# Aggregating the edges of 32 targets in half of the PE's columns, two batches side by side

## The chip, the cores and the metric

The kernel runs on one core of one Trainium2 chip. The metric is the device time of one launch in microseconds (us), the median of several runs. A profile of one execution of the kernel before is at hand. Its engines are called PE (matmul), PEld (PE's weight loads), DVE, ACT, POOL and SP.

## The reference

A gated graph layer over 16 batches (b), 1024 nodes and 256 channels. `adj` is a sparse 1024 x 1024 matrix, used as both A_a and A_m, with some 9 sources u per target v:

```python
pre_u = einsum('bud,dk->buk', h, W1[:d]);  pre_v = einsum('bvd,dk->bvk', h, W1[d:])
S   = sigmoid(relu(pre_u[:, :, None] + pre_v[:, None] + b1) @ W2 + b2)     # per edge (u, v)
a_t = einsum('buv,bud->bvd', S * A_a, h)
m_t = einsum('uv,bud->bvd', A_m, h) * h
z   = beta1 * h + beta2 * (a_t @ Wa + ba) + beta3 * (m_t @ Wm + bm)
```

Only the pairs (u, v) where `adj` is not zero matter, so the kernel works on a list of edges.

## The kernel before

The work is cut into 4 groups of 4 batches (`GB = 4`) and 8 blocks of 128 targets: 32 blocks `k`. A block has two windows of 64 targets (`W`), and the edges of a window lie packed in 5 tiles (`TW`) of 128 slots, one edge per slot and partition. So there are 320 tiles, 10 steps `s` per block.

**Lists.** For each of the 8 target blocks `lists(vt)` loads a 128 x 1024 piece of the transposed matrix (`key`), finds each target's sources, and gives each edge a slot. `ahead` is a matrix of ones and zeros whose product with the counts gives each target its first slot. `LO = [0, 6, 20, 32, 32]` says which 32 targets (`V`) tile j may serve; `since` and `until` bound the slots of each target accordingly. The results are `uidx` (the row to gather), `val` (the edge's weight), `onehot` (which of the tile's 32 targets the slot belongs to) and `whose` (target by slot, written by four DMAs per list from the SP queue). Lists 0 to 2 are made before the first tile, lists 3 to 7 are drawn out over blocks 0 to 4, one piece per step.

**Per tile n.** `fetch` gathers 128 rows of a table in DRAM into one of five buffers: 4 batches of pre_u, then 4 batches of h (8 KB a row). `expand` puts pre_v of each edge's target into PSUM (`pc`). `gate` adds the two on DVE, does relu, the product with W2 and the sum over channels; ACT makes the sigmoid and four weighted copies `left[:, 1 + b]`, beside `left[:, 0]`, the ungated weight (`left_adj`). `aggregate` multiplies: the stationary operand is 128 channels of h of the fetched rows, the moving one the 2 x 32 columns of `left` (ungated and gated). There are 8 such products per tile, 4 batches by 2 halves of the channels, and the sums stand in PSUM as `acc`, channels on partitions.

**Per window and block.** `window_end` copies `acc` to `LT` with two ACT copies, and `times_h` multiplies the ungated half by h on DVE. In the next block's steps 2 to 5 `block_end` multiplies `LT` by Wm and Wa, adds the row of biases and h, and writes the result out.

**Beside that**, PE makes, for later blocks, pre_u rows (`rows`, L319 with w_u) and pre_v with its halves swapped (`halves`, L319 with w_v and L360).

**Order.** The order on each engine is the order in which the code is written: the loop over n at the end issues `aggregate(n - 1)`, then the fetches, then `gate(n)`, `left_adj(n + 1)`, then what is due, a piece of a list, and pieces of `block_end`, `halves` and `rows` at fixed steps s, and last `expand(n + 2)`. Small PSUM results share two buffers "misc"; `pc` has two buffers, `acc` one.

Of the kernel before, what the change touches and what calls it, by code (L numbers as in the profile page):

```python
# [13 lines left out]
P = 128  # L14
# [3 lines left out]
def kernel(  # L18
# [37 lines left out]


    nc = tc.nc
    B, N, D = x.shape
# [10 lines left out]
    V = 32  # L70
    LO = [0, 6, 20, 32, 32]
    RC = 5 + S
# [53 lines left out]
    until = fixed([P, 1], "until")  # L126
    hit = fixed([P, 1], "hit")
    nc.vector.memset(since, 0.0)
    nc.vector.memset(until, float(P))
    for lo in LO[1:]:  # L130
        nc.vector.tensor_scalar(hit, inw, float(lo), float(P), ALU.is_ge, ALU.mult)
        nc.vector.tensor_tensor(until, until, hit, ALU.add)
    for lo in LO[:-1]:
        nc.vector.tensor_scalar(hit, inw, float(lo + V), float(P), ALU.is_ge, ALU.mult)
        nc.vector.tensor_tensor(since, since, hit, ALU.add)

    ahead = fixed([P, P], "ahead")
    nc.vector.tensor_scalar(ahead[:, :W], upto[:, :W], row, None, ALU.is_gt)
    nc.vector.tensor_scalar(ahead[:, W:], upto[:, W:P], row, late, ALU.is_gt, ALU.mult)
    slot_of = fixed([P, NW, TW], "slot_of")  # L140
# [6 lines left out]
    nc.vector.tensor_scalar(ident, upto[:, :P], row, None, ALU.is_equal)  # L147
    place = fixed([P, NW, TW, V], "place")
    for w in range(NW):
        for j in range(TW):  # L150
            nc.vector.tensor_scalar(place[:, w, j, :], upto[:, :V], float(LO[j]), None, ALU.add)
    slot, nth = upto, upto[:, :S]
# [18 lines left out]
    val = const.tile([P, NT * NW, TW], FP, name="val")  # L171
    onehot = const.tile([P, NT * NW, TW, V], mybir.dt.bfloat16, name="onehot")
    whose = const.tile([P, NT * NW, E], mybir.dt.uint8, name="whose")
# [24 lines left out]
    def lists(vt):  # L198
# [21 lines left out]
        pw = aside(vt)  # L220
        nc.tensor.matmul(pw[:, 0:1], ahead, R[:, 0:1], start=True, stop=True)
        yield
        first = R[:, 1:2]
        nc.vector.tensor_copy(first, pw[:, 0:1])
# [4 lines left out]
        nc.vector.scalar_tensor_tensor(held, first, since, held, ALU.is_ge, ALU.mult)  # L229
        nc.vector.tensor_tensor(R[:, 0:1], held, first, ALU.add)  # L230
# [14 lines left out]
        for w, mine in enumerate((soon, late)):  # L245
            nc.vector.tensor_scalar(RR[:, w, :], R, mine, None, ALU.mult)
            for h in range(2):
                nc.sync.dma_start(whose[h * W:(h + 1) * W, vt * NW + w, :], few[w * W:(w + 1) * W])
        pe = aside(vt)
        for j in range(TW):  # L250
# [20 lines left out]
        nc.vector.tensor_scalar(vidx[:, sl].rearrange("p w j -> p (w j)"), k_of, BIG + N, None, ALU.add)  # L271
        nc.vector.tensor_tensor(onehot[:, sl].rearrange("p w j v -> p (w j) v"),  # L272
                                place.rearrange("p w j v -> p (w j) v"),
                                L[:, :, 4:5].to_broadcast([P, M, V]), ALU.is_equal)
        wanted.extend((i, j) for i in range(vt * NW, (vt + 1) * NW) for j in range(TW))
# [186 lines left out]

    marks, pcs, accs, hbs, LTs, lefts = {}, {}, {}, {}, {}, {}

# [20 lines left out]
    def left_adj(n):  # L485
        k, g, vt, w, j = where(n)
        i = vt * NW + w
        lefts[n] = wk.tile([P, 1 + GB, V], FP, name="left")
        nc.scalar.activation(lefts[n][:, 0, :], onehot[:, i, j, :], AF.Copy, scale=val[:, i, j:j + 1])  # L489

    def gate(n):
# [10 lines left out]
        for b in range(GB):  # L502
            nc.scalar.activation(lefts[n][:, 1 + b, :], lefts[n][:, 0, :], AF.Copy, scale=gt[:, b:b + 1])  # L503

    def aggregate(n):
        k, g, vt, w, j = where(n)
        if j == 0:
            accs[n // TW] = psa.tile([P, GB, DC, 2, W], FP, name="acc")
        left, f, acc = lefts.pop(n), fetched[n % NF], accs[n // TW]
        for b in range(GB):  # L510
            for c in range(DC):
                d = GD + b * D + c * P
                nc.tensor.matmul(acc[:, b, c, :, LO[j]:LO[j] + V], f[:, d:d + P], left[:, 0:b + 2:b + 1, :],  # L513
                                 start=(j == 0 and b % 2 == 0 and c == 0), stop=(j == TW - 1),
                                 skip_group_check=True)

    def window_end(q, step):
        k, w = divmod(q, NW)
        acc = accs.pop(q)
        if w == 0:  # L520
            LTs[k] = big.tile([P, GB * DC, 2, P], FP, name="LT")
        LT = LTs[k]
        v = slice(w * W, (w + 1) * W)
        for h in range(2):
            i = slice(h * GB * DC // 2, (h + 1) * GB * DC // 2)
            nc.scalar.copy(LT[:, i, :, v], acc[:, h * GB // 2:(h + 1) * GB // 2].rearrange("p b c k v -> p (b c) k v"))  # L526

        def times_h():
            nc.vector.tensor_tensor(LT[:, :, 0, v], LT[:, :, 0, v],  # L529
                                    hTs[k].rearrange("p b c n -> p (b c) n")[:, :, v], ALU.mult)  # L530
            if w == NW - 1:
                del hTs[k]
        after(step + 1, times_h)

    def block_end(k):
# [3 lines left out]
        for h in range(2):  # L539
            for bb in range(2):  # L540
                step = yield
                if bb == 0:
                    pz = small("pz")
                    add_row(pz, bias_p)
                b = 2 * h + bb
                for i, wt in enumerate((w_m, w_a)):
                    for c in range(DC):
                        nc.tensor.matmul(pz[:, bb * D:(bb + 1) * D], LTs[k][:, b * DC + c, i, :], wt[:, c, :],  # L548
                                         start=False, stop=(i == 1 and c == DC - 1), skip_group_check=True)
# [21 lines left out]
    for n in range(total + T):  # L571
# [19 lines left out]
        if 0 < n < total:  # L591
            next(more, None)
        if s in (2, 3, 4, 5) and 0 < k <= BS:
            if s == 2:
# [134 lines left out]
```

## Time and profile before

| what | value |
|---|---|
| median of 3 runs | 1355.8 us (1355.45 to 1357.64) |
| the profiled execution | 1355.8 us, its span 1353.9 us |
| busy time in the span | PE 1277.7, PEld 1167.6, DVE 1096.4, ACT 753.4, POOL 435.1 us |
| mean granted PE clock | 0.953 |
| moved by DMA | 389.34 MB, 296.70 MB of it by the gathers |

The span runs from the first to the last instruction. Busy time is the time in which at least one instruction of the engine ran. A matmul's recorded duration reaches over the start of the next one, so the pace of PE is read from the chain of work (the work that ended last, followed back), whose pieces do not overlap. In a group of instructions the columns are: line, engine, operation, written and read tiles, shape, count; then busy time in us and the mean of one in ns; then the engine's idle time before them, and what ended most of it.

The slices of the span show three stages: set-up until the first gate at about 90 us; blocks 0 to 4 until about 340 us, with the remaining lists; and an even stretch after that.

```profile
PE   5658999888999999999999999999999999999997
...
DVE  9539789888778888888887888888887888888874
ACT  2325455454556656556655665655655666666652
```

### The profile page before, as it was taken

How to read it: one execution, taken by the hardware profiler on the slowest of the kernel's cores; microseconds unless marked ns; L12 is line 12 of the kernel's file. 1: busy time of each engine (PE TensorE's matmuls, PEld its weight loads, DVE VectorE, ACT ScalarE, POOL GpSimd, SP SyncE). 2: the span in 40 equal slices, each digit the busy share in tenths (PEclk: the TensorE clock that was granted, in tenths of full speed). 3: DMA queues.
4: the chain of work that ended last, by engine and by line, in shares of the span. 5: the costliest groups of instructions: out<-in, count | busy, mean ns of one | idle time of the engine just before them, and what ended most of it. 6: DMA issues, size and time to landing. Idle time of an engine off the chain costs nothing.

```text
span 1353.9 us, 24556 instructions
## 1 busy us (share of the span) xinstructions
PE 1277.7 (94%) x8096; PEld 1167.6 (86%) x8096; DVE 1096.4 (81%) x3413; ACT 753.4 (56%) x2434; POOL 435.1 (32%) x411
## 2 busy tenths in 40 slices
PE   5658999888999999999999999999999999999997
PEld 4548888777999999999999999999999999999986
DVE  9539789888778888888887888888887888888874
ACT  2325455454556656556655665655655666666652
POOL 2047534443432222222222222222222333333320
PEclk9776978898999999999999999999999999999988
DMA  7687867767899998888899998988998888888872
GB/s 225 204 266 248 277 213 231 268 243 262 279 328 323 329 320 306 315 310 303 311 327 329 329 318 307 318 314 298 314 319 291 313 300 298 298 303 309 305 279 73
DMA packets 143304, 389.34 MB, mean 288 GB/s; under 512 B 16336, under 2 KB 101840, under 8 KB 106960
## 3 DMA queue, kind: packets, MB, share of 16 engines
q0 software_dynamic: 48640, 296.70, 62.1%
q1 hardware_dynamic: 75392, 72.62, 16.3%
q10 hardware_dynamic: 19136, 18.35, 4.4%
q8 instruction: 66, 1.08, 0.3%
q14 instruction: 70, 0.57, 0.1%
HBM read 391.69 MB, written 50.33 MB: 326 GB/s over the span
## 4 chain that ended last, share of the span: by engine, by line
PE 66%; DVE 12%; issue 8%; DMA 7%; POOL 3%; ACT 2%; SPq 1%; ACTq 0%; POOLq 0%; DVEq 0%
PE acc L513 29%; PE misc L548 13%; PE misc L319 12%; PE pc L481 8%; DVE t L498 4%; DMA fetched<-table,uidx 4%; DVE t L494 3%; POOL fetched L467 2%; PE misc L323 2%; DMA key<-in_adjT_dram 2%; DVE R L210 1%; POOL val L282 1%; PE misc L360 1%; DMA table<-in_x_dram 1%; ACT LT L526 1%
## 5 line engine op out<-in xcount | busy, mean ns | idle before, releaser
L513 PEld LDWEIGHTS acc<-left,fetched 128*128 128x128 f32 x5120 | 637.0, 196 | 50.6 <-ACT left L503 23.8
L513 PE MATMUL acc<-left,fetched 128*128 128x64 f32 x5120 | 625.2, 277 | 15.4 <-ACT left L503 15.4
L467 POOL DMA_INDIRECT fetched<-table,uidx x320 | 339.8, 1062 | 827.2 <-PE acc L513 613.9
L494 DVE TENSOR_TENSOR t<-fetched,pc 128x1024 f32<-128x1024 f32 x320 | 389.0, 1216 | 130.2 <-PE pc L481 74.2
L498 DVE SCALAR_TENSOR_TENSOR t<-t,w_b 128x256 f32<-128x256 f32 x1280 | 470.3, 422 | 23.9 <-ACT LT L526 0.5
L503 ACT ACTIVATE left<-left,gt 128x32 f32<-128x32 f32 x1280 | 306.5, 310 | 10.4
L481 PE MATMUL pc<-X,mark 128*128 128x512 f32 x640 | 251.9, 475 | 19.6 <-DVE t L494 18.1
L501 ACT ACTIVATE gt<-sc,b_b 128x4 f32<-128x4 f32 x320 | 95.4, 298 | 187.0 <-DVE t L498 186.1
L526 ACT COPY LT<-acc 128x512 f32<-128x512 f32 x128 | 68.7, 589 | 216.5 <-PE acc L513 216.5
L481 PEld LDWEIGHTS pc<-X,mark 128*128 128x128 f32 x640 | 123.0, 196 | 37.5 <-DVE t L494 20.2
L319 PE MATMUL misc<-w_u,hT 128*128 128x256 f32 x512 | 136.5, 416 | 17.8 <-DMA hT<-in_xT_dram 9.5
L548 PE MATMUL misc<-w_m,LT 128*128 128x256 f32 x512 | 140.3, 398 | 1.6 <-DVE LT L529 1.6
L548 PE MATMUL misc<-w_a,LT 128*128 128x256 f32 x512 | 135.9, 389 | 0.0
L319 PEld LDWEIGHTS misc<-w_u,hT 128*128 128x128 f32 x512 | 100.9, 207 | 33.1 <-ACT tab L335 10.1
L319 PE MATMUL misc<-w_v,hT 128*128 128x256 f32 x512 | 122.7, 383 | 0.0
L548 PEld LDWEIGHTS misc<-w_a,LT 128*128 128x128 f32 x512 | 100.5, 196 | 14.5
L319 PEld LDWEIGHTS misc<-w_v,hT 128*128 128x128 f32 x512 | 99.0, 193 | 13.1
L548 PEld LDWEIGHTS misc<-w_m,LT 128*128 128x128 f32 x512 | 96.0, 198 | 12.2 <-DVE LT L529 1.9
L282 POOL DMA_INDIRECT val<-in_adjT_dram,vidx x80 | 85.3, 1066 | 59.6 <-DVE onehot L272 36.1
L498 DVE DVE_READ_ACCUMULATOR t<-t,w_b 128x1 f32 x1280 | 104.0, 81 | 0.0
L335 ACT COPY tab<-misc 128x512 f32<-128x512 f32 x64 | 37.4, 585 | 115.8 <-PE misc L319 101.0
L489 ACT ACTIVATE left<-onehot,val 128x32 f32<-128x32 bf16 x320 | 97.7, 305 | 0.0
(104 smaller groups left out, 662.2 us busy)
## 6 DMA issues: line engine op xcount, KB each, us to landing
hT<-in_xT_dram SPq DMA_DIRECT2D x32, 512.0 KB, 7.7
table<-in_x_dram ACTq DMA_DIRECT2D x32, 512.0 KB, 8.2
table<-tab SPq DMA_DIRECT2D x32, 512.0 KB, 7.9
h_blk<-in_x_dram SPq DMA_DIRECT2D x32, 512.0 KB, 12.7
out_dram<-h_blk SPq DMA_DIRECT2D x32, 512.0 KB, 4.8
fetched<-table,uidx POOLq DMA_INDIRECT x320, 7.5
key<-in_adjT_dram SPq DMA_DIRECT2D x8, 512.0 KB, 9.6
whose<-few SPq DMA_DIRECT2D x32, 40.0 KB, 3.5
```

Source lines behind the costliest of these rows:

```text
L282: nc.gpsimd.indirect_dma_start(out=val[:, i, j:j + 1], out_offset=None, in_=adj_flat, in_offset=bass.IndirectOffsetOnAxis(ap=vidx[:, i, j: ...
L319: nc.tensor.matmul(p[:, bb * D:(bb + 1) * D], hT[:, 2 * h + bb, i, :], wt[:, i, :], start=(i == 0 and not begun), stop=(i == DC - 1), skip ...
L467: nc.gpsimd.indirect_dma_start(out=fetched[n % NF], out_offset=None, in_=table[g], in_offset=bass.IndirectOffsetOnAxis(ap=uidx[:, vt * NW ...
L481: nc.tensor.matmul(pcs[n][:, c], marks[n // TW][:, j * P:(j + 1) * P], cuts[k][:, w, c], start=True, stop=True)
L489: nc.scalar.activation(lefts[n][:, 0, :], onehot[:, i, j, :], AF.Copy, scale=val[:, i, j:j + 1])
L494: nc.vector.tensor_tensor(t, fetched[n % NF][:, :GD].rearrange("p (b d) -> p b d", b=GB), pcs.pop(n).rearrange("p (b d) -> p b d", b=GB), ...
L498: nc.vector.scalar_tensor_tensor(t[:, b, :], t[:, b, :], 0.0, w2_b, ALU.max, ALU.mult, accum_out=sc[:, b:b + 1])
L501: nc.scalar.activation(gt, sc, AF.Sigmoid, bias=b2_b)
L503: nc.scalar.activation(lefts[n][:, 1 + b, :], lefts[n][:, 0, :], AF.Copy, scale=gt[:, b:b + 1])
L513: nc.tensor.matmul(acc[:, b, c, :, LO[j]:LO[j] + V], f[:, d:d + P], left[:, 0:b + 2:b + 1, :], start=(j == 0 and b % 2 == 0 and c == 0), s ...
L526: nc.scalar.copy(LT[:, i, :, v], acc[:, h * GB // 2:(h + 1) * GB // 2].rearrange("p b c k v -> p (b c) k v"))
L548: nc.tensor.matmul(pz[:, bb * D:(bb + 1) * D], LTs[k][:, b * DC + c, i, :], wt[:, c, :], start=False, stop=(i == 1 and c == DC - 1), skip_ ...
```

## The change

1. **Which tiles serve which targets.** The lower 32 targets of a window are packed from slot 0 up and may use tiles 0 to 2; the upper 32 from slot 640 down, tiles 4 to 2. `HALVES` names the halves a tile serves: one, except tile 2, which serves both. `onehot` so has 6 parts of 32 per window in place of 5.
2. **Aggregation.** The operands change places. The stationary one is now 64 columns (32 targets, ungated and gated) of `left`, the moving one 256 channels of a batch. Batches 0 and 1 write partitions 0 to 63 of PSUM (columns 0 to 63 of PE), batches 2 and 3 partitions 64 to 127; they are issued in the order 0, 2, 1, 3. A tile has 4 products, tile 2 has 8. Each half has a PSUM accumulator of its own (`acc0`, `acc1`).
3. **Sums transposed.** The sums now stand with targets on partitions. `half_end` copies an accumulator to SBUF on ACT (`ev`) when its last tile is done; `turn_over` transposes it on PE by four matmuls with the unit matrix into "misc", and ACT copies that to `LT`. This stands at steps 7 (both halves of the first window), 9, and 1 of the next block. `LT` has one buffer in place of two.
4. **Steps moved.** `block_end` runs at steps 3 to 6 in place of 2 to 5, `halves` at 0, 2, 3, 4, 7 in place of 0, 1, 3, 6, 7.
5. **`left`** holds the ungated weights once per batch, beside the gated ones, so that 64 columns lie together; `left_adj` writes 128 columns (256 for tile 2) in place of 32.
6. **The four `whose` DMAs** of a list are issued from ACT's queue in place of SP's.

```diff
-    LO = [0, 6, 20, 32, 32]
+    HALVES = [[0], [0], [0, 1], [1], [1]]
+    OFF = [0, V, 2 * V, 4 * V, 5 * V, 6 * V]
...
+    nc.vector.tensor_scalar(until, upper, float((TW - 1 - MID) * P), float((MID + 1) * P), ALU.mult, ALU.add)
+    nc.vector.tensor_scalar(since, upper, float(MID * P), None, ALU.mult)
+    nc.vector.tensor_scalar(base, upper, float(E), None, ALU.mult)
...
         nc.tensor.matmul(pw[:, 0:1], ahead, R[:, 0:1], start=True, stop=True)
+        nc.tensor.matmul(pw[:, 1:2], below, R[:, 0:1], start=True, stop=True)
...
-                nc.sync.dma_start(whose[h * W:(h + 1) * W, vt * NW + w, :], few[w * W:(w + 1) * W])
+                nc.scalar.dma_start(whose[h * W:(h + 1) * W, vt * NW + w, :], few[w * W:(w + 1) * W])
...
-        lefts[n] = wk.tile([P, 1 + GB, V], FP, name="left")
-        nc.scalar.activation(lefts[n][:, 0, :], onehot[:, i, j, :], AF.Copy, scale=val[:, i, j:j + 1])
+        m = len(HALVES[j])
+        lefts[n] = wk.tile([P, m, GB, 2, V], FP, name=f"left{m}", bufs=3 if m == 1 else 1)
+        nc.scalar.activation(lefts[n][:, :m, :, 0, :],
+                             onehot[:, i, OFF[j]:OFF[j + 1]].rearrange("p (q v) -> p q v", q=m).unsqueeze(2)
+                             .to_broadcast([P, m, GB, V]), AF.Copy, scale=val[:, i, j:j + 1])
...
-        for b in range(GB):
-            for c in range(DC):
-                d = GD + b * D + c * P
-                nc.tensor.matmul(acc[:, b, c, :, LO[j]:LO[j] + V], f[:, d:d + P], left[:, 0:b + 2:b + 1, :],
-                                 start=(j == 0 and b % 2 == 0 and c == 0), stop=(j == TW - 1),
+        for i, q in enumerate(HALVES[j]):
+            first = j == (MID if q else 0)
+            if first:
+                accs[q] = psa.tile([P, 2, D], FP, name=f"acc{q}")
+            for b in (0, 2, 1, 3):
+                half, pair = divmod(b, 2)
+                nc.tensor.matmul(accs[q][half * 2 * V:(half + 1) * 2 * V, pair, :],
+                                 left[:, i, b].rearrange("p k v -> p (k v)"), f[:, GD + b * D:GD + (b + 1) * D],
+                                 start=(first and pair == 0), stop=(j == (TW - 1 if q else MID)),
...
-    def window_end(q, step):
...
+    def half_end(n, q):
+        evs[q] = one.tile([P, 2, D], FP, name=f"ev{q}")
+        nc.scalar.copy(evs[q], accs.pop(q))
+
+    def turn_over(k, w, q, step):
...
+        pt = small("pt")
+        ev = evs.pop(q)
+        for i in range(4):
+            pair, c = divmod(i, DC)
+            nc.tensor.transpose(pt[:, i * P:(i + 1) * P], ev[:, pair, c * P:(c + 1) * P], ident)
+        v = slice(w * W + q * V, w * W + (q + 1) * V)
+        nc.scalar.copy(LT.rearrange("p a c b k v -> p (a c b k) v")[:, :, v], pt.rearrange("p (i v) -> p i v", v=V))
...
-            if n % TW == 0:
-                window_end(n // TW - 1, n)
+            if n % TW in (0, MID + 1):
+                half_end(n - 1, 0 if n % TW else 1)
...
+        if s == 1 and k > 0:
+            turn_over(k - 1, 1, 1, n)
-        if s in (2, 3, 4, 5) and 0 < k <= BS:
+        if s in (3, 4, 5, 6) and 0 < k <= BS:
...
+        if s == 7 and k < BS:
+            turn_over(k, 0, 0, n)
+            turn_over(k, 0, 1, n)
+        if s == 9 and k < BS:
+            turn_over(k, 1, 0, n)
-        if k + 1 < BS and s in (0, 1, 3, 6, 7):
+        if k + 1 < BS and s in (0, 2, 3, 4, 7):
```

**Where instructions stand on PE.** Each row is line, operation, written and read tiles, shape, count; one product is one matmul here. Before, around the middle of a block (fetched0 to fetched4 are the five gather buffers, mark and X the operands of `expand`, LT, w_m and w_a those of `block_end`):

```order
L548 MATMUL misc<-w_m,LT 128x256 x2
L548 MATMUL misc<-w_a,LT 128x256 x2
L481 MATMUL pc<-X,mark 128x512 x2
L513 MATMUL acc<-left,fetched_184 128x2x32 x8
L323 MATMUL misc<-bias_p,unit 128x512
L548 MATMUL misc<-w_m,LT 128x256 x2
L548 MATMUL misc<-w_a,LT 128x256 x2
L481 MATMUL pc<-X,mark 128x512 x2
L513 MATMUL acc<-left,fetched_186 128x2x32 x8
```

After, the last step of `block_end` and step 7 with its transposes (ev and ident), then the tile that serves both halves:

```order
L582 MATMUL misc<-w_m,LT 128x256 x2
L582 MATMUL misc<-w_a,LT 128x256 x2
L500 MATMUL pc<-X,mark 128x512 x2
L537 MATMUL acc_9515<-fetched_173,left_9503 64x256 x4
L556 MATMUL misc<-ident,ev_9420 128x128 x4
L556 MATMUL misc<-ident,ev_9488 128x128 x4
L379 MATMUL misc<-low,swap 128x512
L500 MATMUL pc<-X,mark 128x512 x2
L537 MATMUL acc_9515<-fetched_175,left_9536 64x256 x4
L537 MATMUL acc_9594<-fetched_175,left_9536 64x256 x4
```

Eight products of a tile have become four of another shape, or eight for tile 2, between the same neighbours, and transposes stand at four places of a block.

**On SP's queue**, in blocks 1 and 2 (key is the input of the next list, h_blk and out_0_dram a block's h and result, tab a piece of the gather table). Before:

```order
L555 DMA out_0_dram<-h_blk_623 128x4x256
L248 DMA whose_148<-few_1456 64x640 x4
L200 DMA key_1553<-in_adjT_dram 128x1024
L576 DMA h_blk_1564<-in_x_dram 128x4x256
L336 DMA table1_61<-tab_1505 128x1024
```

After:

```order
L589 DMA out_0_dram<-h_blk_628 128x4x256
L212 DMA key_1554<-in_adjT_dram 128x1024
L610 DMA h_blk_1571<-in_x_dram 128x4x256
L355 DMA table1_61<-tab_1509 128x1024
```

The four `whose` DMAs, which read ACT's `few`, no longer stand between a block's output and the next list's key.

More of the change, by code (lines that the diff above doesn't have):

```diff
@@ L124 @@
     nc.vector.scalar_tensor_tensor(inw, late, -float(W), row, ALU.mult, ALU.add)
[L125 to L139 removed]
+    upper = fixed([P, 1], "upper")
+    nc.vector.tensor_scalar(upper, inw, float(V), None, ALU.is_ge)
+    lower = fixed([P, 1], "lower")
+    nc.vector.tensor_scalar(lower, inw, float(V), None, ALU.is_lt)
+    MID = TW // 2
+    until = fixed([P, 1], "until")
+    nc.vector.tensor_scalar(until, upper, float((TW - 1 - MID) * P), float((MID + 1) * P), ALU.mult, ALU.add)
+    since = fixed([P, 1], "since")
+    nc.vector.tensor_scalar(since, upper, float(MID * P), None, ALU.mult)
+    base = fixed([P, 1], "base")
+    nc.vector.tensor_scalar(base, upper, float(E), None, ALU.mult)
+    ahead = fixed([P, P], "ahead")
+    below = fixed([P, P], "below")
+    hv = fixed([P, 2 * NW, 1], "hv")
+    for q in range(2 * NW):
+        nc.vector.tensor_tensor(hv[:, q, :], late if q // 2 else soon, upper if q % 2 else lower, ALU.mult)
+    nc.vector.memset(below, 0.0)
+    for q in range(2 * NW):
+        c = slice(q * V, (q + 1) * V)
+        nc.vector.tensor_scalar(ahead[:, c], upto[:, c], row, hv[:, q, :], ALU.is_le if q % 2 else ALU.is_gt, ALU.mult)
+        if q % 2:
+            nc.vector.tensor_scalar(ahead[:, c], ahead[:, c], -1.0, None, ALU.mult)
+            nc.vector.tensor_copy(below[:, c], hv[:, q - 1, :].to_broadcast([P, V]))
     slot_of = fixed([P, NW, TW], "slot_of")
@@ L147 @@
     nc.vector.tensor_scalar(ident, upto[:, :P], row, None, ALU.is_equal)
[L148 to L151, printed above, removed]
+    place = fixed([P, 2, V], "place")
+    nc.vector.tensor_copy(place.rearrange("p k v -> p (k v)"), upto[:, :W])
     slot, nth = upto, upto[:, :S]
@@ L221, in lists @@
         nc.tensor.matmul(pw[:, 0:1], ahead, R[:, 0:1], start=True, stop=True)
+        nc.tensor.matmul(pw[:, 1:2], below, R[:, 0:1], start=True, stop=True)
         yield
         first = R[:, 1:2]
-        nc.vector.tensor_copy(first, pw[:, 0:1])
+        nc.vector.tensor_tensor(first, pw[:, 0:1], base, ALU.add)
+        from_ = wk.tile([P, 1], FP, name="from", bufs=2)
+        nc.vector.tensor_tensor(from_, pw[:, 1:2], since, ALU.max)
         held = wk.tile([P, 1], FP, name="held", bufs=2)
@@ L510, in aggregate @@
[L510 to L522 removed]
+        left, f = lefts.pop(n), fetched[n % NF]
@@ new lines, in half_end @@
+    def half_end(n, q):
+        evs[q] = one.tile([P, 2, D], FP, name=f"ev{q}")
+        nc.scalar.copy(evs[q], accs.pop(q))
+    def turn_over(k, w, q, step):
+        if w == 0 and q == 0:
+            LTs[k] = one.tile([P, 2, DC, 2, 2, P], FP, name="LT")
+        LT = LTs[k]
+        pt = small("pt")
[5 more added lines that the diff above has]
+        nc.scalar.copy(LT.rearrange("p a c b k v -> p (a c b k) v")[:, :, v], pt.rearrange("p (i v) -> p i v", v=V))
+        if not q:
+            return
```

34 lines of the change are left out of this document (16 added, 18 removed).

## The prediction

> **What bounds the kernel now.** I read the page's busy times first, then the chain of work, first over blocks 8 to 20 and then piece by piece over one block, and last the groups by line. (Names: a block is 10 gather tiles; there are 32.)
>
> ```profile
> span 1353.9 us, 24556 instructions
> ...
> PE 1277.7 (94%) x8096; PEld 1167.6 (86%) x8096; DVE 1096.4 (81%) x3413; ACT 753.4 (56%) x2434; POOL 435.1 (32%) x411
> ```
>
> ```profile
> 90.00:340.00 250.00, 224.75 (x1246) 199.94 (x1247) 217.08 (x660) 123.86 (x389) 128.45 (x121) 0.84 0.75 250
> 378.00:867.00 489.00, 489.00 (x3244) 453.29 (x3244) 398.76 (x1251) 295.69 (x974) 138.11 (x131) 1.00 0.90 318
> 1056.00:1315.00 259.00, 257.62 (x1728) 238.75 (x1727) 226.01 (x718) 162.49 (x545) 80.69 (x75) 0.98 0.85 303
> ```
>
> The second fence has three windows (length, then busy time of PE, PEld, DVE, ACT, POOL, granted clock, DMA share, GB/s): blocks 0 to 4, blocks 8 to 20 (13 of them, 37.6 us each) and blocks 24 to 31. From 378 us on PE is never idle and DVE is busy 82%; in blocks 0 to 4 PE and DVE share the bound and the clock is 0.84. The chain says the same and prices each kind of PE work:
>
> ```profile
> by line: PE acc L513 45.9%; PE misc L548 18.7%; PE misc L319 18.7%; PE pc L481 12.3%; PE misc L323 3.0%; PE misc L360 1.5%
> ```
>
> ```profile
> 810.28 1.78 PE misc L548 x8
> 812.06 0.46 PE pc L481 x2
> 812.52 1.73 PE acc L513 x16
> 814.25 0.29 PE misc L323
> 814.54 1.73 PE misc L548 x8
> ```
>
> The first fence is the chain of blocks 8 to 20 by line: all of it is PE, and 45.9%, 17.3 us per block, the aggregation at L513. The rows of the second (start, us) are one tile's step. An aggregation costs 1.73 us in 16 records, 108 ns each, for a stream of 64 columns; 8 records of 256 columns (L548) cost 1.73 to 1.78 us, 219 ns each. So four times the columns cost only twice the time: the 64-column record is not paid by its stream.
>
> ```profile
> L513 PEld LDWEIGHTS acc<-left,fetched 128*128 128x128 f32 x5120 | 637.0, 196 | 50.6 <-ACT left L503 23.8
> L513 PE MATMUL acc<-left,fetched 128*128 128x64 f32 x5120 | 625.2, 277 | 15.4 <-ACT left L503 15.4
> ...
> L481 PE MATMUL pc<-X,mark 128*128 128x512 f32 x640 | 251.9, 475 | 19.6 <-DVE t L494 18.1
> ...
> L548 PE MATMUL misc<-w_m,LT 128*128 128x256 f32 x512 | 140.3, 398 | 1.6 <-DVE LT L529 1.6
> ```
>
> 320 tiles times 8 products are 2560, and there are 5120 records: an fp32 product is two loads of 128 columns and two streams. The load is the price of L513.
>
> **The change, part by part.** *Aggregation.* The stationary operand shrinks to 64 columns (32 targets, sum and gated sum), and 256 channels stream. Tiles 0, 1, 3, 4 of a window serve one half, tile 2 both, so a window has 24 products, 48 records, where it had 80. Products alternate between columns 0 to 63 and 64 to 127 of PE. No run of before uses half the columns. If nothing overlaps, a tile costs 8 x 0.219 = 1.75 us and the middle one 3.50; if every pair overlaps, 0.88 and 1.75. In between: the built program puts a product's two records one behind the other, so the order is A A B B C C D D on halves 1 1 2 2 1 1 2 2. If matmuls start in order and one half takes one at a time, the second A overlaps the first B, and so on: 5 slots for 8 records, 9 for 16. That is 1.10 and 1.97 us. I take this one, since every step above starts its records in program order. Per block: 8 x 1.10 + 2 x 1.97 = 12.7 us for 17.3, a gain of 4.6. By the Trainium skill, TensorE: Matmul & The Clock Gate, The mechanism, matmuls in different tiles of the array run at once but keep "strict FIFO, no reordering" among themselves, which would give the same 5 slots.
>
> *Transposes.* 16 of 128 x 128 per block, one load and one matmul each in the built program. Nearest row: the 108 ns load-bound record. Bounds 0.108 and 0.219; I take 0.108, since a 128-column stream is half of the 219 ns one: 1.73 us per block.
>
> *Switching.* Each tile goes from 128-column work to 64-column work and back: 20 switches per block. Below: 0, as between L548 and L481 in the step above, where no time is lost. Above: the next matmul waits for the whole of the one before; the mean record of L548 lasts 398 ns where records follow at 219, so 179 ns; the L513 record gives 277 - 108 = 169. I take the middle, 0.09: 1.8 us per block. The balance is zero at (4.6 - 1.73) / 20 = 0.144 us.
>
> A block so goes from 37.6 to 36.5 us, a gain of 1.07. PE stays the bound in blocks 5 to 31: DVE at 82% of 37.6 is 30.7 us. 27 x 1.07 = 29 us.
>
> *ACT.* L489 writes the value four times wide, the copies of L526 become as many copies of the sums (half_end), and 4 copies of the transposed sums are new.
>
> ```profile
> L489 ACT ACTIVATE left<-onehot,val 128x32 f32<-128x32 bf16 x320 | 97.7, 305 | 0.0
> ```
>
> ```profile
> L526 ACT COPY LT<-acc 128x512 f32<-128x512 f32 x128 | 68.7, 589 | 216.5 <-PE acc L513 216.5
> ```
>
> 4 x 0.589 = 2.4 us, and 10 x at most 0.28 (a 512-wide copy less a 32-wide one): at most 5.2 us on top of 295.69 / 13 = 22.7 in a 36.5 us block. It is hidden by PE's other work; where it is not, it costs a late "left". Transposes share the two "misc" buffers with everything else; step 7 asks for three, and its third waits for ACT's first copy, up to 0.59 us per block if uncovered. The transposed sums arrive a step later and the block's end moves by a step with them: same work. The 4 whole-buffer copies that stood between windows become copies of one half while the other half runs: a gain where it was exposed, at most the 15.4 us above, mostly in blocks 0 to 4.
>
> *DMA.* The four "whose" DMAs per list go from SP to ACT. On SP they wait for ACT's "few", and the next key load is behind them.
>
> ```profile
> SPq L248 <- ACT few L244: 102.3, 6, 29.7
> ```
>
> ```profile
> DVE key L206 <- DMA key<-in_adjT_dram: 13.6, 4, 4.3
> ```
>
> ```profile
> 229.61 2.63 SPq L248 DMA_DIRECT2D whose<-few  x4
> 232.34 0.53 SPq L555 DMA_DIRECT2D out_dram<-h_blk  x1
> 232.93 1.39 SPq L200 DMA_DIRECT2D key<-in_adjT_dram  x1
> ```
>
> With them gone the key starts earlier, and DVE's 13.6 us of idle time can go; ACT takes 2.6 us of issue per list instead, five lists inside blocks 0 to 4, up to 13 us if each delays a "left". Between +13 and -13.6 I take -6, as ACT is half idle there (123.86 of 250) and DVE is not (217.08).
>
> *Setup and lists.* Ten small writes of "place" go; one small matmul and one DVE operation per list and a few more at the start come.
>
> ```profile
> L151 DVE TENSOR_SCALAR place<-upto 128x32 f32<-128x32 f32 x10 | 3.6, 665 | 0.0
> ...
> L221 PE MATMUL misc<-R,ahead 128*128 128x1 f32 x10 | 2.3, 298 | 0.0
> ```
>
> Between -3.6 us and +2.3 us I take nothing.
>
> *The end.* After the last tile the old path was two copies; the new one is one copy, four transposes, one copy: +1 us.
>
> ```profile
> 1334.78 1.08 ACT LT L526 x2
> ...
> 1336.63 6.25 PE misc L548 x16
> ```
>
> Sum: -29 - 6 + 1 = -34. The profiled execution took 1355.8 us around its span of 1353.9, and that is the median of the runs; so 1322 us.
>
> **The rivals.** (1) *Switches cost their upper bound or more.* At 0.18 us a block costs 3.6 in place of 1.8: +0.7, and 27 x 0.73 - 5 = +15, 1371 us. If the load in front of a switch is exposed too (108 ns), 0.29 us, +2.9 per block, 1429. For it: 640 switches stand on the bound, and nothing in the trace shows one. Against it: back-to-back lines of different shape lose nothing. It decides from 0.144 us on. The Trainium skill, TensorEngine Tiling (Array Packing), Key Properties, says that changing the tiling mode "drains the TensorE"; no run here shows it.
>
> (2) *Halves do not overlap.* The aggregation costs 8 x 1.75 + 2 x 3.50 = 21.0 us per block, so +3.7 + 1.7, with or without the 1.8: 27 x 5.4 to 7.2, 1500 to 1550 us. For it: every stream in the trace takes the array alone. Against it: the array does load one product's weights while it streams another's (in the second window 453.29 us of PEld lie beside 489.00 us of PE), so it is not strictly one thing at a time; whether that reaches to two streams no row tells.
>
> (3) *Every pair overlaps.* 8 x 0.88 + 2 x 1.75 = 10.5, a gain of 6.8 - 1.7 - 1.8 = 3.3. Then DMA follows: its share of 0.90 of 37.6 us is 33.8 us of a 34.3 us block; I take 2.5. 1355.8 - 67 - 6 + 1 = 1284. Against it: the order of records.
>
> (4) *The gather ring takes the gain in blocks 24 to 31.* There the chain is no longer all PE:
>
> ```profile
> by line: issue 29.4%; DMA fetched<-table,uidx 15.6%; PE acc L513 13.8%; POOL fetched L467 10.9%; PE misc L548 6.7%; DVE t L498 6.4%; DVE t L494 6.4%; PE pc L481 3.6%; PE misc L319 2.7%; PE misc L323 1.1%; DVE low L352 1.0%; POOLq L467 0.8%;
> ```
>
> Five buffers go round through gate, aggregation, issue and landing. If this loop holds those 8 blocks at their present pace, 8 x 1.07 = 9 us less gain: 1331. It goes with the forecast and lies in its own range.
>
> **How the numbers follow.** Forecast with its own range of 1295 to 1345 (switch 0.04 to 0.14, ring, early blocks): 0.40. Rival 1: 0.26, rival 2: 0.15, rival 3: 0.11; 0.08 for a wait on "misc" or "left" that I do not see, mostly slower. The range from 1275 to 1420 leaves out rival 2 and the far end of rival 1, about 0.2. Faster by over 0.2% (about what a measurement tells from no change): 0.40 + 0.11, and 0.02 of the rest, 0.53. Same: 0.05, out of rival 1 near 0.144 us. Slower: 0.42.
>
> **What would show it.** In the chain of blocks 8 to 20 after: an aggregation piece of 8 records at 1.1 us (0.9: rival 3; 1.75: rival 2), of 16 records at 2.0; transposes x4 at 0.45; a gap or longer first record at each change of columns gives the switch. The key's wait on DVE should be gone, and blocks 0 to 4 shorter by 6 us. The prediction is wrong if records of the two halves start one after the other, if a switch costs over 0.144 us, or if PE idles on ACT's "left" for more than 1 us per block.

## The result, and the profile after

The changed kernel takes 1303.6 us (median of 4 runs, 1301.97 to 1306.39) beside 1355.6 us for the one before: ratio 0.962, 95% interval 0.9595 to 0.9647. It is faster by 52 us where 34 were forecast. The profiled execution took 1306.39 us around a span of 1304.6. The page, as far as it answers to the lines of before:

```profile
span 1304.6 us, 21549 instructions
...
PE 1200.7 (92%) x6576; PEld 800.6 (61%) x6576; DVE 1092.4 (84%) x3418; ACT 870.2 (67%) x2562; POOL 420.3 (32%) x411
...
PE   5747788897999999999999999999999999999996
...
DVE  9639779888888888888888888888888989999993
ACT  2335455565677777777777777777777777777772
```

Weight loads fell from 1167.6 to 800.6 us, PE's busy time by 77 us only, and ACT took 117 us more. The windows say where the time went (length, then busy time of PE, PEld, DVE, ACT, POOL, granted clock, DMA share, GB/s): blocks 0 to 4, the 13 blocks from 374 us on, and blocks 25 to 30.

```profile
87.70:338.00 250.30, 204.65 (x1018) 131.41 (x1019) 217.03 (x669) 139.72 (x406) 128.52 (x120) 0.90 0.74 247
374.00:840.00 466.00, 462.90 (x2630) 311.21 (x2630) 397.35 (x1252) 346.24 (x1029) 129.69 (x131) 1.00 0.95 333
1051.00:1250.00 199.00, 195.59 (x1115) 127.14 (x1112) 180.37 (x575) 151.90 (x461) 60.66 (x60) 1.00 0.89 309
```

Thirteen blocks now take 466 us and took 489: 35.81 us each by the starts of the gates (blocks 8 to 20, every one of them to 0.01), for 37.6, or 37.7 by the starts of the gates. By the starts of each tenth gate (L494 before, L516 after) the spans compare so:

| stage | before, us | after, us | difference |
|---|---|---|---|
| to the first gate | 90.0 | 87.7 | -2.3 |
| blocks 0 to 4 | 249.7 | 250.8 | +1.1 |
| blocks 5 to 23 | 716.7 | 679.1 | -37.6 |
| blocks 24 to 30 | 239.7 | 232.7 | -7.0 |
| block 31 and the end | 57.8 | 54.3 | -3.5 |

The sum is -49.3, the difference of the two spans. Blocks 5 to 23 hold three quarters of it, and there the chain is still PE. By line, over the 13 blocks:

```profile
by line: PE acc L537 33.2%; PE misc L582 20.4%; PE misc L338 19.8%; PE pc L500 13.1%; PE misc L556 5.0%; PE misc L342 4.8%; PE misc L379 2.0%; ACT LT L558 1.7%; issue 0.2%
```

Times 35.81 us, and with the shares of before times 37.6 us, a block's balance is: aggregation 17.3 to 11.9 (-5.4), transposes (L556) +1.8, bias rows (L342) 1.1 to 1.7 (+0.6), the wait for ACT's copy (L558) +0.6, `block_end` (L582) +0.3, the swap (L379) +0.15, the rest +0.2: -1.8. (By the starts of the gates the block falls by 1.9 us.) The bias rows do no more than before; what they hold more is told from the chain's pieces (start, us; tile steps 1 and 2, then step 7):

```profile
811.45 1.01 PE acc L537 x8
812.46 0.59 PE misc L556 x4
813.05 0.47 PE pc L500 x2
813.52 1.01 PE acc L537 x8
814.53 0.43 PE misc L342
814.96 1.73 PE misc L338 x8
816.69 0.46 PE pc L500 x2
817.15 1.88 PE acc L537 x16
...
833.34 0.60 PE misc L556 x4
833.94 0.02 issue
833.96 0.59 ACT LT L558
834.56 0.04 issue
834.60 0.50 PE misc L379
...
837.44 1.92 PE misc L338 x8
```

An aggregation takes 1.01 us where it took 1.73, the middle tile's 1.88. The L342 piece behind it takes 0.43 where L323 took 0.29: the way back to 128 columns is paid in part in the piece that follows. At step 7 the swap (L379) waits until ACT has copied the first transposed sums. PE does the second four transposes meanwhile, so the ACT piece of 0.59 us is not all idle time, and then stands; the timeline of PE shows the idle time after the modelled end of the last transpose in brackets:

```profile
833.27 1.09 PE L556 MATMUL misc<-ident,ev 128*128 128x128 f32 x8
834.60 0.50 PE L379 MATMUL misc<-low,swap 128*128 128x512 f32 x1 [0.24 <-ACT LT L558]
```

By the starts of the records the stop is longer than these 0.24 us: the eight transposes start from 833.27 to 834.09 us, 0.11 us apart but for the first gap, and the swap at 834.60, so PE does nothing new for 0.40 us.

The new groups (busy time, mean ns, idle before):

```profile
L537 PE MATMUL acc<-fetched,left 128*64 128x256 f32 x3072 | 423.5, 397 | 18.4 <-ACT left L526 18.1
L537 PEld LDWEIGHTS acc<-fetched,left 128*64 128x64 f32 x3072 | 202.4, 138 | 211.8 <-issue 53.7
...
L546 ACT COPY ev<-acc 128x512 f32<-128x512 f32 x128 | 75.0, 586 | 78.6 <-PE acc L537 78.6
```

A load now takes 138 ns for 196, and two streams lie beside each other. The starts of the single records, read from the trace, show it: in the tile at 832.26 us they come in four pairs, 5 to 7 ns within a pair, and 0.266, 0.216 and 0.216 us from pair to pair.

### The profile page after: what moved, and what is told of

Read it like the earlier page. It is cut to its first block, busy times and chain, and to the rows that moved or that the text cites. A ratio compares the mean times of both kernels' runs of the same rounds, so it can differ in the third digit from the quotient of the medians.

```text
span 1304.6 us, 21549 instructions
## 1 busy us (share of the span) xinstructions
PE 1200.7 (92%) x6576; PEld 800.6 (61%) x6576; DVE 1092.4 (84%) x3418; ACT 870.2 (67%) x2562; POOL 420.3 (32%) x411
## 4 chain that ended last, share of the span: by engine, by line
PE 71%; DVE 14%; DMA 6%; ACT 4%; issue 3%; ACTq 1%; POOL 1%; SPq 0%; POOLq 0%; DVEq 0%
PE acc L537 24%; PE misc L582 16%; PE misc L338 14%; PE pc L500 9%; DMA fetched<-table,uidx 4%; DVE t L520 4%; DVE t L516 4%; PE misc L342 4%; PE misc L556 3%; DVE R L222 2%; PE misc L379 1%; ACT LT L558 1%; ACT left L526 1%; ACTq L263 1%; DMA key<-in_adjT_dram 1%
## 5 line engine op out<-in xcount | busy, mean ns | idle before, releaser
L486 POOL DMA_INDIRECT fetched<-table,uidx x320 | 321.9, 1006 | 785.9 <-PE acc L537 433.1
L516 DVE TENSOR_TENSOR t<-fetched,pc 128x1024 f32<-128x1024 f32 x320 | 389.1, 1216 | 105.9 <-PE pc L500 76.8
L537 PE MATMUL acc<-fetched,left 128*64 128x256 f32 x3072 | 423.5, 397 | 18.4 <-ACT left L526 18.1
L537 PEld LDWEIGHTS acc<-fetched,left 128*64 128x64 f32 x3072 | 202.4, 138 | 211.8 <-issue 53.7
L526 ACT ACTIVATE left<-left,gt 128x32 f32<-128x32 f32 (+1 forms) x1280 | 313.5, 315 | 10.4
L500 PE MATMUL pc<-X,mark 128*128 128x512 f32 x640 | 246.9, 467 | 22.4 <-DVE t L516 20.7
L500 PEld LDWEIGHTS pc<-X,mark 128*128 128x128 f32 x640 | 118.5, 193 | 44.2 <-DVE t L516 27.0
L338 PE MATMUL misc<-w_u,hT 128*128 128x256 f32 x512 | 129.4, 399 | 16.8 <-DMA hT<-in_xT_dram 8.7
L582 PE MATMUL misc<-w_m,LT 128*128 128x256 f32 x512 | 141.8, 400 | 1.2 <-DVE LT L565 1.2
L582 PE MATMUL misc<-w_a,LT 128*128 128x256 f32 x512 | 133.8, 385 | 0.0
L509 ACT ACTIVATE left<-onehot,val 128x128 f32<-128x128 bf16 (+1 forms) x320 | 130.4, 407 | 0.0
L546 ACT COPY ev<-acc 128x512 f32<-128x512 f32 x128 | 75.0, 586 | 78.6 <-PE acc L537 78.6
L338 PE MATMUL misc<-w_v,hT 128*128 128x256 f32 x512 | 122.6, 383 | 0.0
L338 PEld LDWEIGHTS misc<-w_u,hT 128*128 128x128 f32 x512 | 96.4, 198 | 39.6 <-issue 9.4
L582 PEld LDWEIGHTS misc<-w_m,LT 128*128 128x128 f32 x512 | 94.5, 194 | 34.7 <-issue 22.7
L382 ACT CAST X<-misc 64x512 fp32r<-64x512 f32 x128 | 74.3, 580 | 55.6 <-PE misc L379 51.5
L582 PEld LDWEIGHTS misc<-w_a,LT 128*128 128x128 f32 x512 | 99.4, 194 | 14.0
L338 PEld LDWEIGHTS misc<-w_v,hT 128*128 128x128 f32 x512 | 98.4, 192 | 13.3
```

Of the source, the lines that this page charges most:

```text
L338: nc.tensor.matmul(p[:, bb * D:(bb + 1) * D], hT[:, 2 * h + bb, i, :], wt[:, i, :], start=(i == 0 and not begun), stop=(i == DC - 1), skip ...
L486: nc.gpsimd.indirect_dma_start(out=fetched[n % NF], out_offset=None, in_=table[g], in_offset=bass.IndirectOffsetOnAxis(ap=uidx[:, vt * NW ...
L500: nc.tensor.matmul(pcs[n][:, c], marks[n // TW][:, j * P:(j + 1) * P], cuts[k][:, w, c], start=True, stop=True)
L509: nc.scalar.activation(lefts[n][:, :m, :, 0, :], onehot[:, i, OFF[j]:OFF[j + 1]].rearrange("p (q v) -> p q v", q=m).unsqueeze(2) .to_broad ...
L516: nc.vector.tensor_tensor(t, fetched[n % NF][:, :GD].rearrange("p (b d) -> p b d", b=GB), pcs.pop(n).rearrange("p (b d) -> p b d", b=GB), ...
L526: nc.scalar.activation(lefts[n][:, :m, b, 1, :], lefts[n][:, :m, b, 0, :], AF.Copy, scale=gt[:, b:b + 1])
```

## Experiments

The theory after the result: (a) both halves of PE's columns run fully side by side, whatever the order; (b) a tile's way into 64-column work and back costs 0.26 us, not 0.18. For (b), from single records: the last `pc` record to the first record of the group 326 ns where two `pc` records stand 230 apart, the first gap in the group 266 for 216, the last pair to the next 128-column record 309 for 216: 0.10 + 0.05 + 0.09 = 0.24. The first record behind the group also holds PE 0.03 to 0.05 us longer than it did behind the aggregation before (340 ns for 314 at a bias row, 320 for 272 at a 256-column line), and 166 ns at a transpose, where transposes follow at 109. So the single records give 0.24 us for the way alone and up to 0.30 with the record behind it. The rival to (a): matmuls start in program order, as the prediction had it, and the order 0, 2, 1, 3 is what pairs them. Ratios are to the kernel before on the same chip. A block's length is read from the starts of the gates.

**Order of batches** (`e1_serial`).

```diff
-            for b in (0, 2, 1, 3):
+            for b in (0, 1, 2, 3):
```

> The changed kernel with the products of a tile issued in the order of batches 0, 1, 2, 3, so that the two products of one half of the columns come one behind the other. Same records, same loads, same number of changes between 128 and 64 columns. Theory (two streams run at once when they are in different halves, and start in order): 7 slots of 0.216 us per tile in place of 5, and 13 in place of 9 for the middle tile, so 8 x 0.43 + 2 x 0.86 = 5.2 us more per block, 35.8 to 41.0 in blocks 8 to 20, and some 1445 us in all. Rival (the gain is the smaller load, 64 columns in place of 128 and 48 records in place of 80, and no overlap): no change, 1303 us.

Measured: 1312.0 us, ratio 0.967 [0.963, 0.971], block 35.99 us. Two rows of its chain:

```profile
804.17 1.93 PE acc L537 x16
...
808.49 1.02 PE acc L537 x8
```

With all records of one half ahead of those of the other in the code, the aggregation takes 1.02 us instead of 1.01, and the middle tile 1.93 instead of 1.88, which makes the 0.18 us per block. Start in program order would need 7 slots of 0.216 us. The records still start in four pairs, 12 to 14 ns within a pair. If the records of one pair belong to different halves, a record of the second half starts beside the first half's first one, ahead of records issued earlier, and the in-order account falls. The other rival put on record, that the halves do not overlap and a narrow record is simply cheap, fits these times as well; the next run tells the two apart.

**Half of the aggregation left out** (`e9_onehalf`). Batches 2 and 3 are multiplied only in a half's first tile.

```diff
-            for b in (0, 2, 1, 3):
+            for b in ((0, 2, 1, 3) if first else (0, 1)):
```

> The changed kernel without half of the aggregation: batches 2 and 3 are aggregated only in the first tile of a half, so that in tiles 1, 3 and 4 of a window PE works on columns 0 to 63 alone, with 4 records in place of 8. Theory (the two halves of the columns take their records side by side, 0.21 us for each pair): the 4 records that are left take as long as the 8 did, the aggregation piece stays at 1.0 us and the block at 35.8 us. Rival (a record of 64 columns costs half a record by itself, the halves do not run side by side): the piece falls to 0.55 us, and the block by 8 x 0.43 = 3.4 us.

Measured: block 35.75 us for 35.81 (one run, 1295.8 us). Its chain:

```profile
803.78 1.01 PE acc L537 x4
...
807.41 1.01 PE acc L537 x8
...
813.11 1.87 PE acc L537 x12
```

Four records on one half cost the same 1.01 us as eight on both. They start one at a time, 0.266, 0.216 and 0.216 us apart, where eight start in pairs at the same steps. So the cheap narrow record falls: the second half's work is free here, and one half alone takes its records one at a time. With e1 this settles (a).

**The third "misc" of step 7** (`e3_spread`). The second half of the first window is turned a step later.

```diff
         if s == 7 and k < BS:
             turn_over(k, 0, 0, n)
+        if s == 8 and k < BS:
             turn_over(k, 0, 1, n)
```

> The changed kernel with the second transposition of step 7 moved to step 8, so that step 7 asks for two misc buffers and not three. Theory (the chain shows 0.57 us per block in which PE waits at step 7 for ACT's copy to free a misc buffer, and PE is the bound): 27 x 0.57 = 15 us less, some 1288 us. Rival (the wait moves on to step 8 or 9, where rows asks for misc as well): 1303 us.

Measured: 1299.6 us, ratio 0.956 [0.953, 0.959], block 35.24 us: -0.57. In the chain of steps 7 and 8 no piece of ACT is left:

```profile
833.85 1.01 PE acc L537 x8
834.87 0.59 PE misc L556 x4
835.45 0.23 PE misc L379
835.69 0.47 PE pc L500 x2
836.15 1.88 PE acc L537 x16
838.03 0.59 PE misc L556 x4
```

So the wait was exposed, and is taken away by a line. From the end of the aggregation to `expand` step 7 takes 0.82 us where it took 1.75; step 8 has 0.59 us of transposes more, and the L338 piece behind them takes 1.73 us, as it no longer stands right behind 64-column work, where it took 1.92 (837.44). That is -0.93 + 0.59 - 0.19 = -0.53 of the -0.57; 0.40 of it is PE's standing. The total missed its forecast of 1288 us: the ratio is 0.006, some 8 us, below that of the changed kernel. In the profiles blocks 5 to 23 are 8.5 us shorter and blocks 24 to 30 3.0, and blocks 0 to 4 took 258 us for 251, a difference that the run `again` below weighs.

**No transposes** (`e5_notr`, one run). The copy to `LT` reads `ev` as it stands.

```diff
-            nc.tensor.transpose(pt[:, i * P:(i + 1) * P], ev[:, pair, c * P:(c + 1) * P], ident)
+            pass
...
-        nc.scalar.copy(LT.rearrange("p a c b k v -> p (a c b k) v")[:, :, v], pt.rearrange("p (i v) -> p i v", v=V))
+        nc.scalar.copy(LT.rearrange("p a c b k v -> p (a c b k) v")[:, :, v], ev.rearrange("p a d -> p (a d)").rearrange("p (i v) -> p i v", v=V))
```

> Leaves out the transposes: the copy to LT reads the sums as they stand, so the output has other numbers and every other instruction stays. The three bursts of four per tile pair go from PE, and with them the buffer of misc that step 7 waits for. If a transpose costs its chain price of 0.148 to 0.153 us a burst record (0.59 to 0.60 per four, switch into it included) and the wait of 0.57 us goes too, a block falls from 35.81 by 16 x 0.108 = 1.73 and 0.57 to 33.5 us, or only to some 34.0 us if the transfers stop it first (their share is 0.95 of 35.81). If the transposes stood in time that the two changes of column width cost anyway, only the wait goes: 35.2 us.

Measured: 1266.4 us (on that chip the kernel before took 1368.2 and the changed one, in the run `again` below, 1313.2). Its window over the same 466 us:

```profile
374.00:840.00 466.00, 465.44 (x2563) 307.03 (x2562) 417.17 (x1322) 363.88 (x1088) 136.99 (x139) 1.00 0.99 353
```

Most blocks take 33.70 us: -2.1 where 1.73 + 0.57 = 2.3 was expected. It fits 1.73 for the transposes and the 0.40 us that PE stood. The transfers are not what keeps these blocks at 33.70, since from 607 to 840 us every piece of the chain is PE's. They stop single blocks before that, of up to 34.5 us, with the DMA share at 0.99: a gather stands on the chain for 10.3 us at 433.89. So the transposes cost what the prediction took for them, and the wait comes on top.

**Fewer changes of width, and a sixth gather buffer** (`e6_ring6`, `e7_spread_ring6`, `e8_pairs`). Six buffers in place of five (`t` and `h_blk` give theirs up, and `h_blk` is loaded at step 9 in place of 0) test whether the gather loop holds blocks 24 to 31; e7 is that with the step-7 edit of e3; e8 is e7 with two tiles aggregated back to back in every second step, so 10 changes in and out per block become 5.

```diff
-    NF = 5
+    NF = 6
...
-        t = big.tile([P, GB, D], FP, name="t")
+        t = big.tile([P, GB, D], FP, name="t", bufs=1)
```

```diff
-            aggregate(n - 1)
...
+        if n % 2 == 0 and 2 <= n <= total:
+            for m in (n - 2, n - 1):
+                aggregate(m)
+            for m in (n - 2, n - 1):
+                if m + NF < total:
+                    fetch(m + NF)
```

> The changed kernel with six gather buffers in place of five; to make room the DVE tile t has one buffer (it is written and read by DVE alone) and h_blk one, loaded at step 9 in place of 0. Theory (in blocks 24 to 31 the ring of five gathers holds the block at 33.2 us where PE would need 0.8 us less): 7 us less, 1297 us, with blocks 8 to 20 as they are, 35.8 us. Rival (DMA is full there, share 0.89, not the ring): 1303 us.

> The changed kernel with the second transposition at step 8 and six gather buffers. Theory: 35.24 us in blocks 8 to 20, from the transposition, and 32.5 us in blocks 24 to 31, from the buffers: 27 x 0.57 = 15 us and 8 x 0.7 = 6 us less, 1283 us against 1304. Rival (the two buffers taken from t and h_blk cost in blocks 0 to 4 what the ring gains): 0.956 of before, as with the transposition alone, some 1297 us.

> The changed kernel with the second transposition at step 8, six gather buffers, and the aggregations of two tiles issued one behind the other at every second step, so that PE changes between 128 and 64 columns 10 times per block in place of 20. Theory (the two changes around a tile cost 0.26 us together): blocks 8 to 20 fall from 35.24 us by 5 x 0.26 = 1.3 us to 33.9 us, unless DMA, whose share is 0.95 in a 35.8 us block, stops them at some 34.0 us; 1355 x 0.945 = 1280 us. Rival (changes cost nothing, and the 0.26 us are the latency of the first and last record, hidden elsewhere): 35.2 us per block, and the total as with the second transposition at step 8, 0.956 of before, or above, as buffers come free later.

| kernel | time, us | ratio, interval | blocks 8 to 20 | blocks 24 to 30 | blocks 0 to 4 in its profile |
|---|---|---|---|---|---|
| after | 1303.6 | 0.962 [0.9595, 0.9647] | 35.81 | 33.24 | 250.8 |
| e6_ring6 | 1311.7 | 0.965 [0.962, 0.968] | 35.81 | 32.55 | 263.7 |
| e7_spread_ring6 | 1280.7 | 0.945 [0.943, 0.947] | 35.24 | 32.13 | 247.9 |
| e8_pairs | 1277.3 | 0.941 [0.939, 0.944] | 34.50 | 32.41 | 252.7 |

With the sixth buffer each of the last blocks takes 0.7 us less than in the profile of after, and 0.3 to 0.6 less than in the other profiles with five buffers and the same program in these blocks or nearly so (32.81 to 33.10 in `again`, e1, e2 and e3). e7 has 0.68 less than e3. So the ring does hold them, by 0.3 to 0.7 us. Over the whole launch e6 missed its 1297 us and shows no gain that can be told from after. e7 met its 1283, but it lies 0.011, 15 us, below e3, of which the last blocks give 5; its blocks 0 to 4 were 10 us shorter than e3's in the profiles, and why is open. e8 met its 1280 us in all, but not its 33.9 us per block: it saves 0.74 us beside e7, where 5 x 0.26 = 1.3 was expected. That rules out changes that cost nothing. Its timeline of PE shows two tiles in one group, and what took the rest:

```profile
757.52 1.95 PE L537 MATMUL acc<-fetched,left 128*64 128x256 f32 x16
759.40 0.50 PE L342 MATMUL misc<-b_p,unit 128*128 128x512 f32 x1
...
775.61 0.50 PE L342 MATMUL misc<-bias_p,unit 128*128 128x512 f32 x1 [0.35 <-DVE h_blk L586]
```

Sixteen records take 1.88 us to the next piece (757.52 to 759.40), two tiles apart 2 x 1.01. But once per block PE now waits for a "misc" buffer that DVE's addition of h (L586) frees: 0.35 us after the modelled end of the record before, and 0.51 by the starts, as this L342 starts 746 ns after the last `pc` record where the block's other L342 behind a `pc` record starts after 235. (0.74 + 0.51) / 5 is 0.25 us per change in and out, so (b) is borne out. e8 is the best version measured; its interval touches that of e7, and the last blocks give 0.3 us each back.

**The "whose" DMAs** (`e2_whose_sp`: the changed kernel with them back on SP; `e4_before_act`: the kernel before with them on ACT).

```diff
-                nc.scalar.dma_start(whose[h * W:(h + 1) * W, vt * NW + w, :], few[w * W:(w + 1) * W])
+                nc.sync.dma_start(whose[h * W:(h + 1) * W, vt * NW + w, :], few[w * W:(w + 1) * W])
```

> The changed kernel with the four whose DMAs of a list back on SP's queue. My prediction's term: blocks 0 to 4 get 6 us longer, 1310 us. What the traces suggest now: DVE's wait for the key fell from 13.6 to 6.6 us with the change, but ACT's issues of whose stand on the chain with 7.8 us in blocks 0 to 4, so the move is worth nothing: 1300 to 1306 us.

> The kernel before with nothing but the four whose DMAs of a list moved from SP's queue to ACT's. The prediction's term: 6 us less, in blocks 0 to 4, as the key is loaded earlier. Rival, from the runs so far (whose back on SP made no difference that can be told): within 3 us of before.

Measured: e2 1310.9 us, ratio 0.965 [0.962, 0.968], not to be told from the changed kernel's 0.962; e4 1349.9 us, ratio 0.9953 [0.9935, 0.9970], so 6.4 us less than before. Waits for the key (us in total, times, longest), of e4 and of after:

```profile
DVE key L206 <- DMA key<-in_adjT_dram: 1.8, 1, 1.8
```

```profile
DVE key L218 <- DMA key<-in_adjT_dram: 6.6, 1, 6.6
```

In e4 11.8 of the 13.6 us of waiting are gone, and the launch is 6.4 us shorter. Where these are is not shown: in its profile blocks 0 to 4 take 248.3 us for 249.7, and the time to the first gate is 88.5 for 90.0. In the changed kernel the wait is shorter with the DMAs on either queue (6.5 us in all in e2, 2.5 in `again`), so its fall is not shown to come from the move, and nothing comes of it in the time.

**The changed kernel again** (`again`), for blocks 0 to 4.

> The changed kernel once more, for its first 340 us: blocks 0 to 4 took 250.2 us in its first profile, and 244 to 263 us in the profiles of its variants. If their length is set by the program, it is 250 us again within 1 us; if it moves from run to run, no difference of a few us between single profiles there says anything about an edit.

```profile
87.70:345.00 257.30, 206.16 (x1019) 132.11 (x1019) 217.27 (x669) 140.09 (x407) 128.00 (x120) 0.89 0.73 239
```

The same program took 257.3 us there (profiled time 1313.2 us) where it took 250.3, with the same work on each engine, and blocks 8 to 20 took 35.81 us again. This run was on another chip, where the kernel before took 1368.2 us for 1355.6, so the pair alone does not tell the run from the chip. But on one chip, too, the seven runs of e2 lie between 1300.1 and 1315.9 us, and its profile, with 244 us for blocks 0 to 4, is the fastest of them. So the 244 to 264 us of single profiles do not tell what an edit does there.

## Why the prediction was right, and where it was not

- *Aggregation.* "5 slots for 8 records, 9 for 16" failed: it is 4 and 8. The step behind it, that records start in program order across the halves, is what e1 and e9 contradict; with it falls the strict first-in-first-out rule that the prediction cited from the Trainium skill, TensorE: Matmul & The Clock Gate, The mechanism, as far as two column halves go (8 records in 4 slots in e1). By 0.216 us slots a block's aggregation is 8 x 0.86 + 2 x 1.73 = 10.4 us in place of 12.7: 6.9 gained for 4.6. That is rival 3's mechanism, which had 0.11.
- *Switching* was taken at 0.09 us each; it is 0.12 to 0.15 (0.24 to 0.30 in and out), 2.4 to 3.0 us per block in place of 1.8. That is about the point of 0.144 at which the prediction, with an aggregation of 12.7 us, had no gain left; with the overlap that the halves have, the break-even is (6.9 - 1.73) / 20 = 0.26. That changing the tiling mode drains the array, which the prediction cited from the Trainium skill, TensorEngine Tiling (Array Packing), Key Properties, agrees in kind: 309 ns to the next record for 216. Whether it drains in full the trace does not tell, as the last record's modelled length is 379 ns. That section states no price.
- *Transposes*, 1.73 us per block: eight start from 833.27 to 834.09, 0.108 to 0.110 us apart but for the first gap, and e5's -2.1 with the wait bears it out.
- *The wait at step 7* was named, with "up to 0.59 us per block if uncovered", and stands in the sum at nothing; the only reason near it, "hidden by PE's other work", is said of ACT's added time. It is not hidden: PE stands 0.40 us, and without the wait a block is 0.57 us shorter (e3), some 10 us over the blocks of 35.81 us. Behind it on PE stand the swap, `expand` and the next aggregation, and all three started after it (834.60, 835.10 and 835.57 us in the chain).
- So a block: -6.9 + 1.7 + 2.4 + 0.4 = -2.4 by these terms, or -1.8 with changes at 0.30; -1.8 to -1.9 measured, -1.07 forecast. Two errors, of 0.6 to 1.2 and of 0.4, against the kernel and one of 2.3 for it.
- *Blocks 24 to 31.* Rival 4 held in part: the ring limits them (e6, e7), yet they gained 1.0 us each, near the 1.07 that was summed, of the 1.8 that PE gained elsewhere. After the change the transfers are the second largest piece there:

```profile
by line: PE acc L537 23.2%; DMA fetched<-table,uidx 23.0%; PE misc L582 18.1%; PE pc L500 8.6%; PE misc L338 6.9%; issue 5.7%; DVE t L516 5.0%; PE misc L342 4.3%; DVE t L520 2.7%; POOL fetched L486 2.0%; PE misc L556 1.8%; PE misc L379 1.2%
```

- *Blocks 0 to 4, -6.* The size is that of the whole launch for the kernel before (e4, -6.4), where its own profile puts only 1.4 us in blocks 0 to 4; for the changed kernel it is wrong. The 13.6 us that the term started from are those of the whole span; 9.2 of them lie between 90 and 340 us. In the chain there the key's transfer falls from 7.6% to 4.2% of 250 us (8.5 us), and ACT's issues of the four DMAs, absent before, take 3.1% (7.8 us). Before:

```profile
by line: issue 14.0%; DVE t L498 11.1%; PE acc L513 11.0%; DVE t L494 9.7%; DMA key<-in_adjT_dram 7.6%; PE misc L548 6.3%; POOL val L282 5.6%; DVE R L210 5.1%; PE misc L319 4.3%; PE pc L481 2.5%; ACT left L503 2.2%; ACT LT L526 1.7%; SPq L2
```

After:

```profile
by line: DVE t L520 16.2%; DVE t L516 13.8%; PE acc L537 8.7%; issue 7.7%; DVE R L222 6.0%; PE misc L338 5.2%; DMA key<-in_adjT_dram 4.2%; ACT left L526 3.7%; PE misc L582 3.1%; ACTq L263 3.1%; PE pc L500 3.0%; DMA val<-in_adjT_dram,vidx 1.
```

  That is the price the prediction put as the other end of its bounds. With 7 us between two profiles of one program, how much this decides is open, and so is why PE's smaller load there brings nothing; DVE's two gate lines, 20.8% of the chain before, are 30.0% now.
- *The end*, +1: from the start of the last gate to the end 24.7 us before, 25.1 after, +0.4. Block 31 as a whole gained 3.5, and the time to the first gate 2.3, which the sum had left at nothing; that time was 90.0 and 92.1 us in the profiles of e1 and e2, so the 2.3 are not shown to come from the change. The 15.4 us that the prediction took as the bound on the copies between windows are, in their own row, waits for ACT's `left`; they entered no sum.

The total came 18 us under the forecast because one term was wrong by more than two others together, in its favour. The sign rested on the overlap of the halves, which was right. That the size came no further off was luck: with 5 and 9 slots, the changes and the wait as they were would have left little or nothing of the gain per block (-4.6 + 1.7 + 2.4 + 0.4 = -0.1).

## What to carry to other kernels

A matmul whose time goes into loading its stationary operand gains from changing the operands' places and cutting the stationary one to 64 columns, if two independent sums can stand in the two halves: the second half's records were free here. Count the changes between 64- and 128-column work, 0.24 to 0.30 us in and out here, and put the narrow work together. Before pricing a new step at nothing, count the buffers that it asks for at its place: two in a pool and three requests in a step stopped PE for 0.40 us in every block, and one line mended it.

## What the runs showed of the hardware that was not expected

- Matmuls on columns 0 to 63 and 64 to 127 start side by side at fp32 (5 to 7 ns apart in the tile read above, 12 to 14 in e1), and a record of one half does not wait for earlier-issued ones of the other: 8 records in 1.02 us with all of one half first, 1.01 alternated, and 1.01 for 4 records on one half.
- A 64-column load (138 ns mean, 196 for 128 columns) is hidden: the pairs follow at the 216 ns of their 256-column streams, while 128-column work with 64-column streams went at 108 ns per record. That the loads set that pace fits, since four times the stream took only twice as long, but no run separates them.
- Transposes of 128 x 128 at fp32 follow at 0.108 to 0.110 us, half the 0.216 us of a 256-column record.
